# A four-layer graph network: two stages take their blocks from cold to hot, and the next layer's projection gets a queue

## The chip, the cores and the metric

The kernel runs on one core of one Trainium2 chip. The metric is the device time in microseconds of one execution, as the median of several runs. A profile comes from one profiled execution; its span goes from the first to the last instruction of the program.

The engines in the profile: PE (TensorE, matmuls, with PEld for its weight loads), DVE (VectorE), ACT (ScalarE), POOL (GpSimd, which here issues the gathers) and SP (SyncE, which issues the other DMAs).

## What is computed

A graph of 3327 nodes (padded to 3328), 512 features a node, and a sparse 0/1 adjacency matrix. Four layers, each with a residual: layer norm and ReLU, then

- layer 0: graph attention with 8 heads and a batch norm over the nodes,
- layer 1: SAGE, the mean of the neighbours' rows, two projections and a combination,
- layers 2 and 3: graph attention with 8 heads, then ELU.

One attention layer and SAGE, cut from the reference:

```python
h = jnp.maximum(_layernorm(x, axis=-1), 0.0)
# SAGE
agg = mask @ h / jnp.maximum(deg, 1.0)
x = x + relu(concat([h @ W_self + b_self, agg @ W_nb + b_nb]) @ W_comb + b_comb)
# attention
Wh = jnp.einsum('nd,hdo->hno', h, W)
e = leaky_relu(f1[:, :, None] + f2[:, None, :], 0.2)
e = jnp.where(adj[None, :, :] > 0, e, NEG_INF)
x = x + elu(softmax(e, axis=-1) @ Wh)
```

The expected degree of a node falls as one over the square root of its number: the first nodes have many neighbours, the last ones few.

## The kernel before

The nodes are in 26 blocks of 128, each block in two groups of 64 rows. A group has a fixed number of chunks of 128 neighbours, from the table `CAPS`: 22, 15, 13, 12, 11, 10, 9 for the first groups, down to 6 for groups 19 to 29, 5 for 30 to 50 and 4 for group 51. All together 359 chunks. A block with many chunks is called hot here, one with few cold: block 0 has 37 chunks, blocks 15 to 24 have 10 each, block 25 has 9. Block 25 also holds the padded node, whose row stands for a node without neighbours: it is the mean over all nodes (`mean`, L698 to L700), so every other block's row has to be there before it.

The stages follow one another: lists and the first projection, attention 0, batch norm and the first half of SAGE (`own`), SAGE's sums, attention 2, attention 3. Between layers a table in DRAM is written, one row a node, and a small one (`r_dram`) with a factor a node; the next layer's gathers read the table and can only start when all of it is there.

Attention (`attend`): a group's chunks are taken in units of up to three, 135 units a layer. For each unit POOL gathers rows of the table (L1208, one indirect DMA a chunk), DVE makes the weights in two instructions (L1326 and L1333), then `later()` is called, which moves every group's ending on by one step and calls `tick()`, and then PE multiplies the weights with the rows (L1347). At a group's first unit `fetch` loads the factors of the group after next (L1234, on SP) and `spread` broadcasts those of the next one (L1242, on PE). A group's ending takes a copy, a reciprocal and eight multiplications on ACT (L1285); a block's ends with ELU and the residual (`elu_into`, L1378 to L1384), writes x3 and hands the block to the next layer's projection with `begin`.

SAGE's sums: for each block the chunks of its two groups are taken side by side, two a part; POOL gathers `z_rows`, ACT casts the mask, PE adds up (L1612), with one tick per row of chunks. Its ending (`ending(b, acc)`) takes a transpose (L1555), a projection (L1561), and adds `own`'s result in `y` for that block (L1566).

The next layer's projection (`Following`) runs beside both. A block goes through `norm` (three steps, on ACT in attention 2; in SAGE `norm_by_columns`, two steps) in the list `early`, and then through `rest` (six steps: transposes L883 and ReLU L886; sd L891; wh L904; the row and its store L913, L914; a transpose L917; r_row L920 and its store) or, in SAGE, `rest_by_rows` (five steps, L838 to L873) in the list `ready`. In attention 2 all PSUM results of `rest` share one bank (`pb=1`); in SAGE there are two. How many steps a tick takes:

```python
for _ in range(min(2, len(self.ready))):
    while self.ready and next(self.ready[0]) is None:
        self.ready.pop(0)
self.step()
```

so with two blocks ready it takes two steps, and one that finishes a block goes straight on to the next block's first step. After the last unit `hurry` gives the projection spare PSUM banks (those of `mx`), and two blocks move on at a time until all are done.

In both attentions the order on PE, DVE and ACT is that in which the program records its instructions (`manual_schedule`); in SAGE a scheduler orders them. Blocks are taken in the order 0 to 25 everywhere.

Of the kernel before, what the change touches and what calls it, by code (L numbers as in the profile page):

```python
# [23 lines left out]
F32 = mybir.dt.float32  # L24
# [14 lines left out]
P = 128  # L39
H = 8  # L40
F = 64
D = H * F
# [414 lines left out]
class Products:  # L457
# [117 lines left out]
class Projection:  # L575
# [165 lines left out]
class Following:  # L741

    def __init__(self, tc, cs, N, wl, W, WA, table, r_dram, pool, psum, pb=1, ab=None):

        self.__dict__.update(locals())
        nc = tc.nc
        if ab is not None:
            self.ab = pool.tile([P, 2, D], F32, name=f"ab{wl}")  # L750
            for k, a in enumerate(ab):
                nc.sync.dma_start(self.ab[:, k, :], a.partition_broadcast(P))
        self.NB = table.shape[0] // P
        self.Wt = pool.tile([P, KC, D], F32, name=f"fWt{wl}")
        nc.sync.dma_start(self.Wt, W.rearrange("(kc p) o -> p kc o", p=P))
        self.hs = pool.tile([P, self.NB, KC], F32, name=f"hs{wl}")
        self.early, self.ready, self.spare = [], [], None

    def begin(self, c, xt):
        self.early.append((self.norm_by_columns if self.spare is not None or self.ab is not None else self.norm)(c, xt))  # L760

    def busy(self):
        return self.early or self.ready

    def hurry(self, spare):

# [7 lines left out]
    def tick(self):  # L774
        if self.spare is not None:
            for g in self.ready[:2]:
                if next(g) is None:
                    self.ready.remove(g)
            self.step()
            return  # L780
        for _ in range(min(2, len(self.ready))):
            while self.ready and next(self.ready[0]) is None:
                self.ready.pop(0)
        self.step()

    def step(self):
        for g in list(self.early):
            hx = next(g)
            if hx is not None:
                self.early.remove(g)  # L790
                self.ready.append((self.rest if self.ab is None else self.rest_by_rows)(*hx))

    def drain(self):
        while self.early or self.ready:
            self.tick()

    mean = Projection.mean
# [382 lines left out]
def sparse(ctx: ExitStack, tc: tile.TileContext, t: dict, out: bass.AP, WA, ls, cs, idx, rdeg, first):  # L1180
# [17 lines left out]
    x2 = dram.tile([NP, D], F32, name="fx2")  # L1198
    x3 = dram.tile([NP, D], F32, name="fx3")
# [10 lines left out]
        )  # L1210


    def attend(layer, table, r_dram, finish, tick=lambda: None, home=None, beside=None):

# [1 line left out]

        width = table.shape[1]
        units = []  # L1220
        for g in range(ls.G):
            mine = list(ls.batches(g, UNIT))
            units += [(g, k0, n, i == 0, i == len(mine) - 1) for i, (k0, n) in enumerate(mine)]
        hq = H // PG
        sw = hq * (F + 1)
        with tc.tile_pool(name=f"fatt{layer}", bufs=2) as ap, tc.tile_pool(
            name=f"facc_ps{layer}", bufs=2, space=PSUM
# [1 line left out]
            rows, rrs, rbs, accs, ends, over = {}, {}, {}, {}, [], []  # L1229

            def fetch(g):
                if g < ls.G:
                    rr = ap.tile([2, H * GB], F32, name="r_two", tag="r_two", bufs=3)
                    nc.sync.dma_start(rr, r_dram[g, :, :, :].rearrange("t h i -> t (h i)"))  # L1234
                    rrs[g] = rr

            def spread(g):


                if g < ls.G:  # L1240
                    rb = aps.tile([P, H * GB], F32, name="r_bc", tag="r_bc", bufs=2)
                    nc.tensor.matmul(rb, ones[0:2, :].bitcast(F32R), rrs.pop(g).bitcast(F32R), start=True, stop=True)  # L1242
                    rbs[g] = rb.rearrange("p (h i) -> p h i", i=GB)
# [50 lines left out]
                        ends.remove(e)  # L1294
                tick()

            for g in range(2):
                fetch(g)
            spread(0)
            def load(i):  # L1300

                if i >= len(units):
# [18 lines left out]
            for i, (g, k0, n, begins, stops) in enumerate(units):  # L1321
                gt = rows.pop(i)
                mk = mask[:, k0 : k0 + n, :]
                full = [P, n, H, GB]
                mx = aps.tile([P, UNIT, H, GB], F32, name="mx", tag="mx", bufs=1)
                nc.vector.tensor_tensor(  # L1326
                    mx[:, :n],
                    rbs[g].unsqueeze(1).to_broadcast(full),
                    gt[:, :n, H * (F + 1) : ROW].unsqueeze(3).to_broadcast(full),
                    ALU.max,  # L1330
                )
                wt = ap.tile([P, UNIT, H, GB], F32, name="wgt", tag="wgt", bufs=3)
                nc.vector.tensor_tensor(wt[:, :n], mx[:, :n], mk.unsqueeze(2).to_broadcast(full), ALU.mult)  # L1333
                load(i + 1)
                later()
                if begins:
                    fetch(g + 2)
                    acc = aps.tile([P, BANK], F32, name="facc", tag="acc")
                    accs[g] = acc
                    spread(g + 1)  # L1340

                for k in range(n):
                    f, l = begins and k == 0, stops and k == n - 1
                    for q in range(hq):
                        for v in range(PG):
                            h = q * PG + v
                            nc.tensor.matmul(  # L1347
                                accs[g][v * GB : (v + 1) * GB, q * (F + 1) : (q + 1) * (F + 1)],
                                wt[:, k, h, :],
                                gt[:, k, h * (F + 1) : (h + 1) * (F + 1)],  # L1350
                                start=(f and q == 0),
                                stop=(l and q == hq - 1),
                            )
                if stops:
                    ends.append(ending(g))
            over.append(True)
            if beside is not None:
                mx = aps.tile([P, UNIT, H, GB], F32, name="mx", tag="mx", bufs=1)
# [1 line left out]
            while ends or (beside is not None and beside.busy()):  # L1360
                later()

    def following(lx, layer, wl, W, pb=1, ab=None):
# [5 lines left out]
        return Following(tc, cs, N, wl, W, WA, table, r_dram, pp, pps, pb, ab)  # L1369
# [24 lines left out]
    with ExitStack() as mx:  # L1394
# [107 lines left out]
        with tc.tile_pool(name="fln", bufs=1) as bp:  # L1502
# [40 lines left out]
            for i in range(2):  # L1543
                own(NB - 2 + i)

        proj = following(mx, 2, 1, t["L2_gnn_W"], 2, (t["L2_gnn_a1"], t["L2_gnn_a2"]))
        ends = []

        def ending(b, acc):
# [26 lines left out]


        parts = []
        for b in range(NB):
            ps = list(zip_longest(*(list(ls.batches(b * PG + u, SUNIT)) for u in range(PG))))  # L1580
            parts += [(b, p, i == 0, i == len(ps) - 1) for i, p in enumerate(ps)]
        loaded = {}
# [18 lines left out]
        for i, (b, _, begins, stops) in enumerate(parts):  # L1601
# [4 lines left out]
            for r, u, k, m, z in loaded.pop(i):  # L1606
# [3 lines left out]
                g = b * PG + u  # L1610
# [101 lines left out]
```

## Time and profile before

| what | value |
|---|---|
| median of 3 runs | 2906.87 us (2898.61 to 2909.07) |
| span of the profiled execution | 2535.3 us |
| around the span | 371.6 us (difference of the two) |
| PE, DVE, ACT, POOL busy | 73%, 75%, 39%, 56% of the span |
| gathers of SAGE | 919.7 to 1399.0 us |
| units of attention 2 (first L1326 to last L1333) | 1450.4 to 1989.8 us |
| units of attention 3 | 2040.5 to 2513.7 us |

The busy share of an engine over the whole span mixes stages with different limits: each stage has to be read by itself, and the two attentions, which do the same work but for the projection beside the first of them, can be compared unit by unit. In a timeline line the brackets at the end tell how long the engine was idle before it and what ended that.

### The profile page before, as it was taken

How to read it: one execution, taken by the hardware profiler on the slowest of the kernel's cores; microseconds unless marked ns; L12 is line 12 of the kernel's file. 1: busy time of each engine (PE TensorE's matmuls, PEld its weight loads, DVE VectorE, ACT ScalarE, POOL GpSimd, SP SyncE). 2: the span in 40 equal slices, each digit the busy share in tenths (PEclk: the TensorE clock that was granted, in tenths of full speed). 3: DMA queues.
4: the chain of work that ended last, by engine and by line, in shares of the span. 5: the costliest groups of instructions: out<-in, count | busy, mean ns of one | idle time of the engine just before them, and what ended most of it. 6: DMA issues, size and time to landing. Idle time of an engine off the chain costs nothing. (4 is left out here: it accounts for less than half of the span.)

```text
span 2535.3 us, 53563 instructions
## 1 busy us (share of the span) xinstructions
PE 1848.6 (73%) x21112; PEld 1172.1 (46%) x21112; DVE 1901.8 (75%) x2355; ACT 996.7 (39%) x3581; POOL 1427.6 (56%) x1508
## 2 busy tenths in 40 slices
PE   3767756777667698889999667778787746565764
PEld 2444434554444242223333265656555435555654
DVE  7667579999999951233444499999877479999997
ACT  3554212334455431223333114567766501233443
POOL 1000167778776026777776277766555077777663
PEclk9778889988888899999999768898887786778566
DMA  8774188887776566777887478888666178788784
GB/s 327 275 272 132 43 273 281 274 280 217 237 237 196 203 216 203 235 247 256 260 258 243 122 219 239 240 234 238 210 185 198 56 217 234 235 238 244 234 239 129
DMA packets 189056, 562.56 MB, mean 222 GB/s; under 512 B 37764, under 2 KB 42304, under 8 KB 185470
## 3 DMA queue, kind: packets, MB, share of 16 engines
q0 software_dynamic: 115456, 404.86, 53.8%
q1 hardware_dynamic: 73342, 154.20, 17.1%
q8 instruction: 169, 2.77, 0.4%
q14 instruction: 89, 0.73, 0.1%
HBM read 499.26 MB, written 59.68 MB: 220 GB/s over the span
## 5 line engine op out<-in xcount | busy, mean ns | idle before, releaser
L1208 POOL DMA_INDIRECT rows<-table,idx x1077 | 1032.1, 958 | 558.1 <-issue 220.0
L1347 PE MATMUL facc<-rows,wgt 128*64 128x65 f32 x17232 | 744.1, 256 | 346.4 <-DVE wgt L1333 241.2
L1347 PEld LDWEIGHTS facc<-rows,wgt 128*64 128x64 f32 x17232 | 690.0, 168 | 484.5 <-DVE wgt L1333 292.8
L1326 DVE TENSOR_TENSOR mx<-r_bc,rows 128x1536 f32<-128x1536 f32 (+1 forms) x405 | 639.2, 1578 | 40.9 <-DMA rows<-table,idx 23.5
L1333 DVE TENSOR_TENSOR wgt<-mx,mask 128x1536 f32<-128x1536 f32 (+1 forms) x405 | 638.4, 1576 | 41.9 <-ACT bn_y L1285 0.5
L1208 POOL DMA_INDIRECT z_rows<-h_dram,idx x359 | 343.2, 956 | 230.8 <-PE h_ps L1530 94.7
L1285 ACT ACTIVATE fhp<-sums,rd 64x64 f32<-64x64 f32 x816 | 216.0, 336 | 304.1 <-DVE rd L1279 300.8
L1612 PE MATMUL sage_acc<-z_rows,z_mask 128*64 128x512 f32 x718 | 220.2, 620 | 30.8 <-DMA z_rows<-h_dram,idx 30.7
L1318 ACT ACTIVATE mask<-on 128x192 uint8<-128x192 uint16 (+1 forms) x135 | 46.7, 346 | 326.2 <-DVE on L1312 292.7
L849 DVE TENSOR_TENSOR sd_pr<-p_wh,ab 128x1024 f32<-128x1024 f32 x26 | 31.9, 1225 | 187.6 <-PE p_wh L846 187.6
L1129 POOL DMA_DIRECT2D list_b<-shift x12 | 6.0, 506 | 271.7 <-DVE shift L1083 271.5
L1593 ACT CAST z_mask<-mask 128x128 f32<-128x128 uint8 (+1 forms) x196 | 52.8, 287 | 205.3 <-PE sage_acc L1612 204.2
L1612 PEld LDWEIGHTS sage_acc<-z_rows,z_mask 128*64 128x64 f32 x718 | 52.4, 138 | 157.7 <-issue 87.5
L681 PE MATMUL wh_ps<-fWt,hT 128*128 128x512 f32 x208 | 123.5, 749 | 0.0
L1285 ACT ACTIVATE bn_y<-sums,rd 64x64 f32<-64x64 f32 x408 | 107.6, 334 | 1.9
L846 PE MATMUL p_wh<-fWt,hT 128*128 128x512 f32 x208 | 98.6, 618 | 2.1 <-DVE hT L700 1.9
L904 PE MATMUL p_wh<-fWt,hT 128*128 128x512 f32 x184 | 99.9, 691 | 0.0
L1242 PE MATMUL r_bc<-r_two,fones 2*128 2x512 f32 x156 | 94.8, 611 | 7.0 <-DMA r_two<-r_dram 3.4
L1275 ACT COPY sums<-facc 128x260 f32<-128x260 f32 x153 | 55.8, 365 | 105.5 <-PE facc L1347 65.9
L1561 PE MATMUL n_ps<-fWx,aT 128*128 128x512 f32 x208 | 96.8, 605 | 0.2 <-ACT aT L1557 0.2
L1535 PE MATMUL s_ps<-fWx,hT 128*128 128x512 f32 x208 | 93.6, 603 | 3.5 <-ACT hT L1532 3.5
L1044 PE MATMUL words_ps<-wsel,adj_b 128*128 128x8 bf16 x676 | 24.8, 168 | 88.7 <-DVE adj_b L1026 48.4
(232 smaller groups left out, 2146.5 us busy)
## 6 DMA issues: line engine op xcount, KB each, us to landing
adj_i<-in_adj SPq DMA_DIRECT2D x26, 1664.0 KB
table<-v_row SPq DMA_DIRECT2D x78, 264.0 KB
rows<-table,idx POOLq DMA_INDIRECT x1077
fin_x<-fx SPq DMA_DIRECT2D x52, 256.0 KB
ln_x<-in_x SPq DMA_DIRECT2D x26, 256.0 KB
bn_x<-in_x SPq DMA_DIRECT2D x13, 512.0 KB
fx<-bn_x SPq DMA_DIRECT2D x13, 512.0 KB
fsage_x<-fx SPq DMA_DIRECT2D x26, 256.0 KB
```

Source lines behind the costliest of these rows:

```text
L681: nc.tensor.matmul(wh, hT[:, kc, :], self.Wt[:, kc, :], start=(kc == 0), stop=(kc == KC - 1))
L846: nc.tensor.matmul(wh, hT[:, kc, :], self.Wt[:, kc, :], start=(kc == 0), stop=(kc == KC - 1))
L904: nc.tensor.matmul(wh, hT[:, kc, :], self.Wt[:, kc, :], start=(kc == 0), stop=(kc == KC - 1))
L1208: nc.gpsimd.indirect_dma_start(out=dst, out_offset=None, in_=src[:, :], in_offset=bass.IndirectOffsetOnAxis(ap=idx[:, k : k + 1], axis=0))
L1242: nc.tensor.matmul(rb, ones[0:2, :].bitcast(F32R), rrs.pop(g).bitcast(F32R), start=True, stop=True)
L1285: nc.scalar.mul(hp[o0 : o0 + GB, h * F : (h + 1) * F], sm[mine, q, 0:F], rd[mine, q, :])
L1326: nc.vector.tensor_tensor(mx[:, :n], rbs[g].unsqueeze(1).to_broadcast(full), gt[:, :n, H * (F + 1) : ROW].unsqueeze(3).to_broadcast(full), ...
L1333: nc.vector.tensor_tensor(wt[:, :n], mx[:, :n], mk.unsqueeze(2).to_broadcast(full), ALU.mult)
L1347: nc.tensor.matmul(accs[g][v * GB : (v + 1) * GB, q * (F + 1) : (q + 1) * (F + 1)], wt[:, k, h, :], gt[:, k, h * (F + 1) : (h + 1) * (F + 1)],
L1535: nc.tensor.matmul(ps, hT[:, kc, :], Wx[:, 0, kc, :], start=(kc == 0), stop=(kc == KC - 1))
L1561: nc.tensor.matmul(ps, aT[:, kc, :], Wx[:, 1, kc, :], start=(kc == 0), stop=(kc == KC - 1))
L1612: nc.tensor.matmul(acc[u * GB : (u + 1) * GB, :], m, z, start=f, stop=l)
```

## The change

Three things. The blocks of SAGE's sums and of the second attention are taken in the order 24, 23, ..., 0, 25. The projection takes at most two blocks at a time: others wait in a queue and are loaded again from DRAM (`late_x`) when their turn comes. And a tick takes one step of the first ready block only, without going on into the next; attention adds one more step behind the matmuls of every third unit (`beside.onward()`). Attention 0 and attention 3 keep their order.

```diff
+        self.waiting, self.loaded = [], []
 
     def begin(self, c, xt):
+
+        if self.waiting or self.loaded or len(self.early) + len(self.ready) > 1:
+            self.waiting.append(c)
+        else:
+            self.normed(c, xt)
+
+    def normed(self, c, xt):
         self.early.append((self.norm_by_columns if self.spare is not None or self.ab is not None else self.norm)(c, xt))
 
+    def refill(self):
+
+        if self.loaded and len(self.early) + len(self.ready) < 2:
+            self.normed(*self.loaded.pop(0))
+        if self.waiting and not self.loaded:
+            c = self.waiting.pop(0)
+            xt = self.pool.tile([P, D], F32, name="late_x", tag="late_x", bufs=2)
+            self.tc.nc.sync.dma_start(xt, self.xin[c * P : (c + 1) * P, :])
+            self.loaded.append((c, xt))
...
-            self.step()
-            return
-        for _ in range(min(2, len(self.ready))):
-            while self.ready and next(self.ready[0]) is None:
-                self.ready.pop(0)
+        else:
+            self.onward()
         self.step()
+        self.refill()
+
+    def onward(self):
+
+        if self.ready and next(self.ready[0]) is None:
+            self.ready.pop(0)
...
+    late = [*range(NB - 2, -1, -1), NB - 1]
...
-        for g in range(ls.G):
+        order = [b * PG + u for b in blocks for u in range(PG)]
+        after = dict(zip(order, order[1:]))
+        for g in order:
...
-                    fetch(g + 2)
+                    fetch(after.get(after.get(g)))
...
-                    spread(g + 1)
+                    spread(after.get(g))
...
+                if beside is not None and i % 3 == 0:
+                    beside.onward()
...
-        for b in range(NB):
+        for b in late:
...
-        proj = following(l3, 3, 2, t["L3_gnn_W"])
-        attend(2, at2.table, at2.r_dram, elu_into(x2, x3, proj.begin), proj.tick, beside=proj)
+        proj = following(l3, 3, 2, t["L3_gnn_W"], x3)
+        attend(2, at2.table, at2.r_dram, elu_into(x2, x3, proj.begin), proj.tick, beside=proj, blocks=late)
```

More of the change, by code (lines that the diff above doesn't have):

```diff
@@ L741, with __init__ @@
 class Following:
-    def __init__(self, tc, cs, N, wl, W, WA, table, r_dram, pool, psum, pb=1, ab=None):
+    def __init__(self, tc, cs, N, wl, W, WA, table, r_dram, xin, pool, psum, pb=1, ab=None):
         self.__dict__.update(locals())
@@ L757, in __init__ @@
         self.early, self.ready, self.spare = [], [], None
+        self.waiting, self.loaded = [], []
     def begin(self, c, xt):
-        self.early.append((self.norm_by_columns if self.spare is not None or self.ab is not None else self.norm)(c, xt))
+        if self.waiting or self.loaded or len(self.early) + len(self.ready) > 1:
[3 more added lines that the diff above has]
+    def normed(self, c, xt):
+        self.early.append((self.norm_by_columns if self.spare is not None or self.ab is not None else self.norm)(c, xt))
+    def refill(self):
[6 more added lines that the diff above has]
+            self.loaded.append((c, xt))
     def busy(self):
-        return self.early or self.ready
+        return self.early or self.ready or self.waiting or self.loaded
     def hurry(self, spare):
@@ L793, in drain @@
     def drain(self):
-        while self.early or self.ready:
+        while self.busy():
             self.tick()
@@ L1210, in gather, with attend @@
         )
-    def attend(layer, table, r_dram, finish, tick=lambda: None, home=None, beside=None):
+    late = [*range(NB - 2, -1, -1), NB - 1]
+    def attend(layer, table, r_dram, finish, tick=lambda: None, home=None, beside=None, blocks=range(NB)):
         width = table.shape[1]
         units = []
-        for g in range(ls.G):
+        order = [b * PG + u for b in blocks for u in range(PG)]
+        after = dict(zip(order, order[1:]))
+        for g in order:
             mine = list(ls.batches(g, UNIT))
@@ L1231, in fetch @@
             def fetch(g):
-                if g < ls.G:
+                if g is not None:
                     rr = ap.tile([2, H * GB], F32, name="r_two", tag="r_two", bufs=3)
@@ L1237, in spread @@
             def spread(g):
-                if g < ls.G:
+                if g is not None:
                     rb = aps.tile([P, H * GB], F32, name="r_bc", tag="r_bc", bufs=2)
@@ L1295, in later @@
                 tick()
-            for g in range(2):
+            for g in order[:2]:
                 fetch(g)
-            spread(0)
+            spread(order[0])
             def load(i):
@@ L1361, in attend, with following @@
                 later()
-    def following(lx, layer, wl, W, pb=1, ab=None):
+    def following(lx, layer, wl, W, xin, pb=1, ab=None):
         table = dram.tile([NP, ROW], I32, name=f"table{layer}")
@@ L1368, in following @@
         pps = lx.enter_context(tc.tile_pool(name=f"fproj_ps{layer}", bufs=1, space=PSUM))
-        return Following(tc, cs, N, wl, W, WA, table, r_dram, pp, pps, pb, ab)
+        return Following(tc, cs, N, wl, W, WA, table, r_dram, xin, pp, pps, pb, ab)
     def elu_into(xin, dst, then=lambda c, xt: None):
@@ L1544, in sparse @@
                 own(NB - 2 + i)
-        proj = following(mx, 2, 1, t["L2_gnn_W"], 2, (t["L2_gnn_a1"], t["L2_gnn_a2"]))
+        proj = following(mx, 2, 1, t["L2_gnn_W"], x2, 2, (t["L2_gnn_a1"], t["L2_gnn_a2"]))
         ends = []
```

## The prediction

> **What bounds the kernel now.** I read the page, then the busy time by stretch, then the waits of the stretch where the vector engine falls back, and the timeline of one such block. The span is 2535.3 us, the median of the runs 2906.87; the other 371.6 us lie around the span. No part of the change touches them, so I take differences in the span over to the median one to one.
>
> ```profile
> DVE  7667579999999951233444499999877479999997
> ```
>
> Each digit is 63.4 us. The second run of 9s (slices 23 to 27, counted from 0) is attention 2, the third (33 to 38) attention 3; the 8, 7, 7, 4, 7 between them are the hole to look at. By stretch:
>
> ```profile
> core 0: us, PE busy (x) PEld busy (x) DVE busy (x) ACT busy (x) POOL busy (x), PEclk, DMA share, GB/s
> 1740.00:1800.00 60.00, 48.78 (x721) 36.65 (x716) 56.09 (x60) 45.06 (x178) 38.25 (x40) 0.87 0.80 235
> ...
> 1860.00:1920.00 60.00, 48.79 (x632) 35.48 (x629) 44.82 (x55) 42.18 (x167) 30.98 (x32) 0.77 0.62 188
> ...
> 1980.00:2040.00 60.00, 37.81 (x227) 22.35 (x227) 17.67 (x44) 23.50 (x107) 5.80 (x7) 0.73 0.19 69
> 2400.00:2460.00 60.00, 42.84 (x711) 36.74 (x709) 58.36 (x53) 25.52 (x84) 41.98 (x45) 0.64 0.80 235
> ```
>
> The second and the last row are the same work, the coldest blocks, in attention 2 and in attention 3. Attention 3 holds VectorE at 58.4 of 60 us; attention 2 only at 44.8, and no other engine is full. From the starts of L1326 (135 units a layer) each block's period follows: blocks 15 to 24 take 13.7 us in attention 3 and 18.0 to 19.5, mean 18.75, in attention 2; blocks 10 to 14 take 15.8 and 16.8; blocks 0 to 9 together 246.2 and 254.8. So a projection beside costs about 1 us a block where VectorE is the bound (its own small VectorE instructions: 0.15 + 0.27 + 0.16 + 0.17 + 0.16 = 0.91 us), and 5 us in the cold blocks. What is waited for there:
>
> ```profile
> PEld p_ps L883 <- ACT r_row L920: 25.5, 10, 2.7
> ...
> ACT v_row L913 <- PE p_wh L904: 22.3, 10, 2.9
> DVE s_col L901 <- ACT s_col L898: 20.9, 10, 2.5
> ACT v_row L895 <- PE p_sd L891: 18.9, 10, 2.0
> ```
>
> Ten of each, one a block: a ring through PE and ACT, not a full engine. One turn of it:
>
> ```profile
> 1865.95 0.24 ACT L920 COPY r_row<-p_tr 16x128 f32<-16x128 f32 x1
> ...
> 1866.24 1.12 PE L883 MATMUL p_ps<-fident,ln_h 128*128 128x128 f32 x4 [2.51 <-ACT r_row L920]
> ...
> 1868.59 1.89 PE L891 MATMUL p_sd<-WA,hT 128*128 128x16 f32 x8 [1.23 <-ACT hT L886]
> ...
> 1878.87 1.75 ACT L913 ACTIVATE v_row<-p_wh,v_row 128x64 f32<-128x64 f32 x8 [2.86 <-PE p_wh L904]
> ```
>
> r_row, the transposes and sd stand in one tick: with two blocks ready, tick finishes one generator and goes straight on into the next. PE sits in front of attention's matmuls for 2.51 and then 1.23 us, and everything up to the third wgt buffer backs up. The end of attention 2:
>
> ```profile
> 2003.72 6.55 PE L904 MATMUL mx<-fWt,hT 128*128 128x512 f32 x8 [2.45 <-ACT s_col L898]
> ...
> 2014.76 6.16 PE L904 MATMUL mx<-fWt,hT 128*128 128x512 f32 x8 [0.61 <-ACT r_row L920]
> ...
> 2024.90 3.70 PE L904 MATMUL mx<-fWt,hT 128*128 128x512 f32 x8 [0.61 <-ACT r_row L920]
> ```
>
> Three blocks' projections are still to do after the last unit (1989.8), 10.1 to 11.0 us apart; the next layer's first unit starts at 2040.50, 50.7 us later. SAGE:
>
> ```profile
> 1398.08 0.95 POOL L1208 DMA_INDIRECT z_rows<-h_dram,idx  x1 [1.95 <-PE p_tr L869]
> ...
> 1412.26 1.07 PE L1612 MATMUL sage_acc<-z_rows,z_mask 128*64 128x512 f32 x2
> ```
>
> A gather costs GpSimd 0.95 + 0.30 = 1.25 us, and 359 of them make 450 us: this is the pace of SAGE's hot blocks. The cold ones turn PE-bound: the gathers of blocks 20 to 24 are 14.2 us apart instead of 12.5, so PE reaches the last gather's rows 14.2 us after its issue, and the table is complete 28 us after that (write at 1440.46).
>
> **What the Trainium skill says.** "TensorE: Matmul & The Clock Gate", The mechanism: matmuls start and end in strict order. The trace agrees: attention's matmuls stand behind the waiting p_ps. The same page, What's actually happening: the array runs at half clock after about 3.4 us idle and needs as long busy to get back. The trace shows the two speeds (eight matmuls of L904 in 6.55 or 3.70 us, 48 of L1347 in 2.87 or 1.62), so a stall costs more than itself; my forecast uses only these durations. "Trace Analysis", Optimization Strategy: regimes with different contended engines can be interleaved. That is what is tried here, and the window table shows the regimes.
>
> **Part by part, attention 2.** Removed: the double step of tick. In cold blocks before, the steps of four units go 1, 1, 1, 3 (counted from the code: six steps of rest a block, four units). Now it is one a unit plus one behind every third unit's matmuls, 4.5 units a block. A block arrives every 4 units for blocks 24 to 10, every 5 to 13 later, so the queue grows to about four blocks, is at its worst around block 9 and empty by block 4. In the built program's order p_ps always has matmuls of attention between it and p_sd; p_sd and p_wh stand next to each other about once in nine units, where the extra step meets the next tick.
>
> If all 135 units ran at VectorE's pace: attention 3's 473.2 us, 2.5 for the slower first block, and 24 to 25 projections at about 0.95 = 24; sum 500, against 539.4 now. For the remaining stalls: 6 to 7 of 26 sd steps fall on the extra place and make VectorE wait for s_col, nothing to 2.5 us each (the longest such wait shown), so 0 to 16; I take 7, as PE often has the time. 507, a gain of 32. Bounds: 40 (no stall), and 18 if cold blocks only reach 17.0 as the 6-cap blocks do now (10.5 x 1.75).
>
> The projection's PE and ACT work is not less, only moved; in a cold block PE was busy 15.2 us of 18.75 at clock 0.77, ACT 13.2. With 4/4.5 of a projection a block and a warmer clock both fit under 15. That is the cover, and it is thin; without it the 17.0 above holds.
>
> Added: loads of late_x. The order of the built program has 13, all of x3 in attention 2; SAGE gets none, since there five steps meet five ticks a block. 13 x 256 KB is 3.4 MB beside the 200 GB/s moved: hidden. Each waits on SP until the store just issued has landed (a write to a dependent gather took 3.3 us at 1440.46), and behind it stand the r_two fetch, fin_x, the table and r_dram writes. The fetch leads its use by one group, 6.9 us, so I count nothing; with no cover it is 13 x 3 = 39 us. A gain is excluded, nothing is removed there.
>
> **The end of attention 2.** Blocks 0 and 25 are left instead of 23, 24 and 25: the queue is empty through block 0's 13 units. One round of 10 us goes, and PE no longer trails by some 4 us (last facc matmuls ended about 1994.7). Bounds 8 and 14, I take 12. Next in line are block 0's and then block 25's p_wh, unchanged.
>
> **SAGE.** Cold first meets PE while it still has own's matmuls (8.9 us for two blocks, until 961.9). Before, block 0's 37 gathers without any ending let it catch up. Now after 962 some 93 chunks of 5-cap blocks follow, first 13 us light, then at 14.4 a block, and five 6-cap blocks at 15.6: PE at about 1168 there with POOL 13 chunks ahead, and 186 gathers left x 1.254 = 233: last gather about 1401, against 1399. The end gains: a gather's rows can be used about 4 us after its issue (the third gather of attention 2 at 1446.28, its unit at 1450.36), not 14; 10 less 2 is 8. Bounds: 20 gained (the early deficit is absorbed by the buffers), 8 lost (each cold block at 15.5).
>
> Sum: 32 + 12 + 8 = 52 us. 2535.3 becomes 2483, the median 2855.
>
> **Rivals.**
> - Full cover: 40 + 14 + 20 = 74, 2833. For it: six-cap blocks already run within 1 us of VectorE's pace with the 1, 1, 1, 3 pattern. Against: PE and ACT near 13 to 15 us of a 14.7 us block.
> - Half: cold blocks at 17.0, 18 + 10, SAGE 4 lost: 24, 2883. For it: a single PSUM bank (pb=1) keeps the six steps serial.
> - The queue does nothing: the change of order only moves the same stalls to the front, with 10 from the end given back in SAGE: 2900 to 2910. Against it: the program's order shows the p_ps, p_sd pair broken up.
> - Slower: the serial ring through that bank gets longer instead, because each step now waits behind the endings' eight multiplications (2.14 us) on ACT. The queue is then never empty for some 81 units (from the ninth to block 5), each held at ring / 4.5. Blocks 24 to 5 take 369 us now; at a ring of 21.5 us it is 81 x 4.78 + 31 = 418, 49 more, less 20 from the ends: 2936. It decides from 20.7 us on (slower by over 14.5). Now it is 18.75 with a stall of 3.7 in it.
>
> **How the numbers follow.** Forecast 0.52, full cover 0.15, half 0.20, nothing 0.06, slower 0.07. About 0.5% (14.5 us) can be told from no change. Faster 0.87, same 0.06, slower 0.07. The range of 8 in 10 reaches just past full cover and half: 2831 to 2888.
>
> **What would show it.** Right: VectorE above 56 of 60 us in every stretch of attention 2; the 135 units in 500 to 512 us; cold blocks at 14.7 to 15.6; p_ps no longer waiting for r_row by 2.5 us; two L904 groups on mx instead of three, 38 us from last to first unit; SAGE's last gather near 1401 and the last table write near 1432. Wrong: cold blocks at 17 or more, r_bc waiting for r_two behind a late_x load, or SAGE's gathers ending after 1410.

## The result, and the profile after

The changed kernel takes 2909.88 us (median of 20 runs, 2884.17 to 2923.03), the kernel before 2896.53 (20 runs, 2886.26 to 2909.07). The ratio is 1.0035, 95% interval 1.0018 to 1.0053: no gain, and within the 0.5% that the prediction calls no change. 2855 was forecast.

The profile of the changed kernel has a span of 2893.1 us, and the execution it was taken from took 2894.95: next to nothing lies around the span. The profile before had 2535.3 against runs of 2906.87. That is the first thing to explain. The busy digits of VectorE of the changed kernel, each 72.3 us:

```profile
DVE  7758487787787814333321567777776677878886
```

There is no run of 9s any more, not even in attention 0 (slices 5 to 12) and attention 3 (32 to 39), which the change doesn't touch. Attention 3 takes 572.0 us (from its first L1326, here L1351, to the end of its last L1333, here L1358); it was 474.5 in the profile before. By stretch, the changed kernel, two stretches of the coldest blocks in attention 2, one of its hot blocks, one of attention 3's coldest blocks (columns as before: length, busy time and instructions of each engine, PE's clock, share of the DMA engines, GB/s):

```profile
core 0: us, PE busy (x) PEld busy (x) DVE busy (x) ACT busy (x) POOL busy (x), PEclk, DMA share, GB/s
1660.00:1720.00 60.00, 47.99 (x549) 35.28 (x548) 40.71 (x48) 31.68 (x123) 30.56 (x33) 0.69 0.63 179
1720.00:1780.00 60.00, 43.50 (x513) 29.58 (x513) 41.88 (x49) 37.32 (x144) 30.50 (x32) 0.82 0.69 195
...
2200.00:2260.00 60.00, 47.86 (x673) 34.76 (x671) 46.72 (x38) 15.32 (x60) 28.41 (x30) 0.73 0.56 155
2720.00:2780.00 60.00, 43.54 (x602) 34.27 (x602) 49.35 (x45) 22.99 (x74) 36.21 (x38) 0.68 0.71 199
```

VectorE has 41 of 60 us in the cold blocks, and 49 even where no projection runs beside it. What PE waits for tells more. The groups of instructions of PE, attention's matmuls (busy time and mean of one; idle time before them and what ended it), first of the profile before, then of the changed kernel:

```profile
L1347 PE MATMUL facc<-rows,wgt 128*64 128x65 f32 x17232 | 744.1, 256 | 346.4 <-DVE wgt L1333 241.2 <-issue 81.3 <-ACT sums L1275 18.1
```

```profile
L1372 PE MATMUL facc<-rows,wgt 128*64 128x65 f32 x17232 | 970.5, 264 | 443.7 <-issue 407.9 <-DVE wgt L1358 26.3 <-PE r_bc L1267 1.7
```

"Issue" is idle time for which the profile shows no reason. PE waited 241 us for VectorE's weights before and 26 after, and 408 us for nothing visible. Two of the prediction's own signs did come. In attention 2 p_ps no longer waits for r_row: 0.4 us of PE's idle time in all, 31.4 in the profile before. And two rounds of L925 (L904 before) are left at the end. The timeline of the changed kernel:

```profile
2277.92 4.76 PE L925 MATMUL mx<-fWt,hT 128*128 128x512 f32 x8
2284.68 3.70 PE L925 MATMUL mx<-fWt,hT 128*128 128x512 f32 x8 [1.21 <-DVE v_row L929]
```

### The profile page after: what moved, and what is told of

Same layout as the page of the kernel before. It is cut to its first block, busy times and chain, and to the rows that moved or that the text cites. A ratio compares the mean times of both kernels' runs of the same rounds, so it can differ in the third digit from the quotient of the medians.

```text
span 2893.1 us, 53569 instructions
## 1 busy us (share of the span) xinstructions
PE 2096.7 (72%) x21112; PEld 1315.7 (45%) x21112; DVE 1895.4 (66%) x2354; ACT 999.9 (35%) x3589; POOL 1423.8 (49%) x1508
## 5 line engine op out<-in xcount | busy, mean ns | idle before, releaser
L1372 PE MATMUL facc<-rows,wgt 128*64 128x65 f32 x17232 | 970.5, 264 | 443.7 <-issue 407.9
L1372 PEld LDWEIGHTS facc<-rows,wgt 128*64 128x64 f32 x17232 | 820.4, 173 | 666.2 <-issue 593.7
L1358 DVE TENSOR_TENSOR wgt<-mx,mask 128x1536 f32<-128x1536 f32 (+1 forms) x405 | 638.4, 1576 | 154.9 <-PE facc L1372 71.1
L1351 DVE TENSOR_TENSOR mx<-r_bc,rows 128x1536 f32<-128x1536 f32 (+1 forms) x405 | 639.5, 1579 | 132.8 <-PE facc L1372 88.0
L1639 PE MATMUL sage_acc<-z_rows,z_mask 128*64 128x512 f32 x718 | 206.2, 623 | 7.2 <-DMA z_rows<-h_dram,idx 7.2
L925 PE MATMUL p_wh<-fWt,hT 128*128 128x512 f32 x192 | 127.9, 826 | 20.9 <-ACT s_col L919 11.8
L1588 PE MATMUL n_ps<-fWx,aT 128*128 128x512 f32 x208 | 109.7, 658 | 30.8 <-issue 25.4
L867 PE MATMUL p_wh<-fWt,hT 128*128 128x512 f32 x208 | 104.5, 649 | 10.6 <-issue 6.8
L1593 DVE TENSOR_TENSOR s_o<-n_ps,bn_y 128x512 f32<-128x512 f32 x26 | 17.9, 688 | 130.7 <-PE n_ps L1588 62.0
```

What stands on the lines that cost most here:

```text
L867: nc.tensor.matmul(wh, hT[:, kc, :], self.Wt[:, kc, :], start=(kc == 0), stop=(kc == KC - 1))
L925: nc.tensor.matmul(wh, hT[:, kc, :], self.Wt[:, kc, :], start=(kc == 0), stop=(kc == KC - 1))
L1351: nc.vector.tensor_tensor(mx[:, :n], rbs[g].unsqueeze(1).to_broadcast(full), gt[:, :n, H * (F + 1) : ROW].unsqueeze(3).to_broadcast(full), ...
L1372: nc.tensor.matmul(accs[g][v * GB : (v + 1) * GB, q * (F + 1) : (q + 1) * (F + 1)], wt[:, k, h, :], gt[:, k, h * (F + 1) : (h + 1) * (F + 1)],
L1588: nc.tensor.matmul(ps, aT[:, kc, :], Wx[:, 1, kc, :], start=(kc == 0), stop=(kc == KC - 1))
L1639: nc.tensor.matmul(acc[u * GB : (u + 1) * GB, :], m, z, start=f, stop=l)
```

## The experiments

Eighteen runs in five sets; the kernels of one set ran on one chip, beside runs of the kernel before there. Ratios are to those runs.

### First: what the profile before was worth, and the two halves apart

`before_again` is the kernel before; `after_again` the changed one. `steps_only` keeps the queue and the single steps and takes the old order in both stages; `order_only` has the new order and the old projection.

```diff
# steps_only, against the changed kernel
-    late = [*range(NB - 2, -1, -1), NB - 1]
+    late = [*range(NB)]
# order_only, against the changed kernel
     def begin(self, c, xt):
-        if self.waiting or self.loaded or len(self.early) + len(self.ready) > 1:
-            self.waiting.append(c)
-        else:
-            self.normed(c, xt)
+        self.normed(c, xt)
...
-        else:
-            self.onward()
+            self.step()
+            return
+        for _ in range(min(2, len(self.ready))):
+            while self.ready and next(self.ready[0]) is None:
+                self.ready.pop(0)
         self.step()
-        self.refill()
...
-                if beside is not None and i % 3 == 0:
-                    beside.onward()
```

> The kernel before, unchanged, profiled once more. Its first profile has a span of 2535 us beside runs of 2897 us; the changed kernel's has 2893 us beside 2910 us. Theory A (the first profile caught an execution in which PE issued its instructions without pauses, and the timed runs are not like it): span 2870 to 2900 us, PE idle on 'issue' before attention's matmuls some 400 us instead of 81 us, attention 3's units 560 to 580 us instead of 473 us. Theory B (360 us of every run lie around the span): span about 2535 us again, the same 81 us of issue.

> The changed kernel, unchanged, beside the one before on the same chip. Theory A: span 2880 to 2910 us again, or near 2490 us if this execution happens to be one without the pauses; ratio of the runs 1.002 to 1.006. Theory B: span as in its first profile, 2893 us, with almost nothing around it, which B cannot explain for one kernel and not the other.

> The queue and the single steps, with the blocks in the old order 0 to 25 in SAGE and attention 2. If the single steps are what was worth having (the ring through one PSUM bank, as predicted), this is 10 to 30 us below before, less the projections left over at the end (the queue is longest there, one to two blocks more, +10 to +20 us): 2885 to 2905 us. If PE's issue is the bound (theory A), the steps save nothing and the longer end remains: 2905 to 2925 us.

> The new order in SAGE and attention 2, with the old double steps and no queue. By the prediction the end of attention 2 is worth 8 to 14 us and SAGE about 8, the cold blocks nothing: 2875 to 2890 us. If SAGE with the cold blocks first costs more than its end gives back, it is 2900 to 2920 us, and the loss shows between the first gather of z_rows and the last one against before_again.

| run | median us | ratio to before (2867.91), interval |
|---|---|---|
| before_again | 2863.51 | 0.9986 [0.9971, 1.0002] |
| after_again | 2872.88 | 1.0018 [1.0000, 1.0036] |
| steps_only | 2872.23 | 1.0009 [0.9994, 1.0025] |
| order_only | 2849.47 | 0.9919 [0.9883, 0.9955] |

The profile of before_again has a span of 2871.4 us and looks like the changed kernel's: theory A of before_again. The same group of PE there:

```profile
L1347 PE MATMUL facc<-rows,wgt 128*64 128x65 f32 x17232 | 969.9, 264 | 416.2 <-issue 378.8 <-DVE wgt L1333 27.4 <-ACT sums L1275 1.0
```

The timeline of PE in attention 3 of before_again, and below it that of the first profile:

```profile
2716.30 1.91 PE L1347 MATMUL facc<-rows,wgt 128*64 128x65 f32 x26
2718.43 0.50 PE L1347 MATMUL facc<-rows,wgt 128*64 128x65 f32 x4 [0.22 <-issue]
2719.17 0.52 PE L1347 MATMUL facc<-rows,wgt 128*64 128x65 f32 x4 [0.23 <-issue]
```

```profile
2410.46 4.60 PE L1347 MATMUL facc<-rows,wgt 128*64 128x65 f32 x80 [0.98 <-issue]
...
2417.89 1.87 PE L1347 MATMUL facc<-rows,wgt 128*64 128x65 f32 x48 [2.11 <-issue]
```

In the first profile a unit's 48 matmuls go through in one piece. In before_again PE takes four, stands still, and takes four more 0.74 us later; some 26 matmuls on it runs freely again. I call these stops pauses. Between two of attention's matmuls (idle time of 0.15 to 1.3 us) there are 58, 48 us in all, in the first profile, and 741, 353 us in all, in before_again. So the profile that the prediction was worked out from came from an execution unlike the timed ones. On which chip it and the first timed runs were taken is not on record.

The stages (us), from the timelines: SAGE from its first gather to attention 2's first unit, attention 2 from first L1326 to the end of the last L1333, from there to attention 3, attention 3.

| run | SAGE | attention 2 | to attention 3 | attention 3 |
|---|---|---|---|---|
| before_again | 610.1 | 631.7 | 47.0 | 561.2 |
| changed, first profile | 612.0 | 642.8 | 34.8 | 572.0 |
| after_again | 621.3 | 626.2 | 38.2 | 562.0 |
| steps_only | 597.8 | 608.9 | 72.4 | 561.1 |
| order_only | 626.1 | 601.6 | 35.4 | 562.0 |

Either half alone shortens attention 2 by 23 to 30 us; both together by 5.5 in the same set. steps_only gives its 23 us back at the end of attention 2 (72.4 against 47.0). order_only gains what was expected of it, but not where: 30 us in attention 2, where nothing was put down for the cold blocks, and SAGE is 16 longer. These are single executions, and the two of the changed kernel are 17 us apart in attention 2, so only the larger differences count.

### Second: where the changed kernel loses it, and SAGE

`att_order` is order_only with SAGE in the old order. `mix` adds single steps in SAGE alone. `mid_extra` and `clip_moved` are the changed kernel with one edit each: the extra step stands between the first and the second chunk of the unit, not behind its matmuls; VectorE's clip of s_col moves from the step of wh to the start of the step after it.

```diff
# att_order, against order_only
-        for b in late:
+        for b in range(NB):
# mix, against att_order (in tick)
+        if self.ab is not None:
+            self.onward()
+            self.step()
+            return
# mid_extra, against the changed kernel
                 for k in range(n):
+                    if beside is not None and i % 3 == 0 and k == 1:
+                        beside.onward()
...
-                if beside is not None and i % 3 == 0:
-                    beside.onward()
# clip_moved, against the changed kernel
-        nc.vector.tensor_scalar(sf, sf, -SMALL, SMALL, ALU.max, ALU.min)
...
+        nc.vector.tensor_scalar(sf, sf, -SMALL, SMALL, ALU.max, ALU.min)
```

> The kernel before with the new order in attention 2 alone; SAGE keeps 0 to 25, double steps, no queue. Theory A (the gain of the order lies in attention 2 and at its end, SAGE only gives back): against order_only SAGE's 16 us come back. From the stage times of before_again and order_only: attention 2 30 us shorter, its end 12 shorter, SAGE unchanged: 42 us less than before, ratio 0.985, about 2825 where before is 2868. Theory B (SAGE's order moves only what waits, its loss and attention 2's gain are one and the same delay): no better than order_only, ratio 0.992.

> att_order with single steps in SAGE alone (the double steps stay in attention 2, no queue). Theory A (steps_only's 12 us in SAGE come from the single steps there and do not depend on the order): another 10 to 12 us less than att_order, ratio 0.981, about 2813. Theory B (the 12 us were the queue's, which holds blocks back from SAGE's scheduler, or only the spread of single executions): equal to att_order within 0.3%.

> The changed kernel with the extra step of every third unit placed between the unit's first and second chunk instead of behind its matmuls, so that sd and wh do not stand next to each other on PE. Theory A (the neighbourhood of sd and wh, and VectorE's wait for s_col behind it, eat what single steps bring): attention 2 in 600 to 615 us instead of 626 to 643, ratio to before 0.990 to 0.995. Theory B (the queue is the cost: it moves projections from cold blocks to hot ones where each costs more): attention 2 stays at 625 to 640, ratio about 1.002.

> The changed kernel with VectorE's clip of s_col taken one step later, at the start of the step after wh, so that VectorE meets it a unit after sd was issued. Theory A (VectorE's in-order wait for s_col, 82 us idle in after_again against 44 in order_only, is what costs): attention 2 15 to 25 us shorter than in the changed kernel, ratio to before 0.993 to 0.997. Theory B (VectorE only waits there because PE is late anyway; without this wait it waits at the weights' buffers instead): attention 2 within 5 us of the changed kernel's, ratio about 1.002.

The kernel before took 2533.23 us on this chip, and the profiles have no pauses (55 to 65 stops of the kind counted above).

| run | median us | ratio to before, interval |
|---|---|---|
| att_order | 2488.35 | 0.9822 [0.9808, 0.9835] |
| mix | 2488.99 | 0.9822 [0.9808, 0.9837] |
| mid_extra | 2482.45 | 0.9794 [0.9778, 0.9809] |
| clip_moved | 2481.46 | 0.9794 [0.9780, 0.9807] |

All numbers expected were for a chip with pauses, so the first reading is only this: what keeps the changed kernel at 1.00 there may be missing here, or the two edits may have removed it. att_order and mix are equal, in SAGE too (529.2 and 530.6 us): without pauses, single steps bring SAGE nothing. Whether steps_only's 12 us in SAGE were theirs with pauses stays open.

### Third: the changed kernel itself, on a chip without pauses

> The changed kernel unchanged, on whatever chip this call gets. Theory A (there are two kinds of chip: in one PE pauses between instructions all the time and before takes 2860 to 2910 us, in the other it does not and before takes 2533; the sizes of the prediction were those of the second kind): on a chip without the pauses the span is 2480 to 2490, ratio 0.978 to 0.984, attention 2 505 to 512 us, its end 35 us, SAGE 8 to 12 shorter; on a chip with the pauses the ratio is 1.000 to 1.006 again. Theory B (mid_extra and clip_moved were so much faster because of their edits): ratio about 1.00 on either kind.

> att_order again. On a chip with the pauses theory A (the order of attention 2 alone gains, SAGE's order gives back 16 us there): ratio 0.983 to 0.988, about 10 to 16 us ahead of order_only; theory B (SAGE's loss is attention 2's gain in another place): equal to order_only. On a chip without the pauses: 0.982 again.

> mid_extra again, to be set against the changed kernel on the same chip. Theory A (the extra step next to wh makes VectorE wait): on a chip with the pauses 15 to 30 us faster than after_2 (ratio 0.990 to 0.995); on a chip without them the waits are short and it is equal to after_2 within 5 us. Theory B (the queue is the cost): equal to after_2 on either kind.

> The new order in SAGE and attention 2 with the old double steps and no queue. On a chip without the pauses: attention 2 as in att_order, 500 us, its end 36 to 39, SAGE 9 to 12 shorter as in mid_extra: ratio 0.978 to 0.981, so that single steps and queue bring nothing (theory A); theory B (they bring what is missing): behind after_2 by 5 us or more. On a chip with the pauses: 0.992 again, ahead of after_2 by 0.8 to 1.2%.

Another chip, before 2531.00 us, no pauses.

| run | median us | ratio, interval | SAGE | attention 2 | to attention 3 |
|---|---|---|---|---|---|
| before (first profile) | | | 530.7 | 540.8 | 49.4 |
| after_2 | 2483.53 | 0.9812 [0.9799, 0.9826] | 519.2 | 514.7 | 34.5 |
| att_order_2 | 2485.27 | 0.9827 [0.9813, 0.9842] | 529.0 | 506.8 | 35.6 |
| mid_extra_2 | 2474.97 | 0.9784 [0.9769, 0.9800] | 518.7 | 508.7 | 34.7 |
| order_only_2 | 2471.34 | 0.9757 [0.9743, 0.9771] | 518.0 | 506.7 | 35.3 |

This decides it: the change as it stands is 1.9% faster here, 47.5 us, which is theory A of after_2 (its attention 2, 514.7 us, is a little over the 505 to 512 expected), and the edits of mid_extra and clip_moved weren't the reason. The windows of after_2 (columns as above), the coldest blocks of attention 2 and, last, its hot end:

```profile
1460.00:1520.00 60.00, 45.27 (x704) 34.97 (x705) 57.52 (x69) 46.90 (x177) 45.56 (x47) 0.85 0.84 254
...
1820.00:1880.00 60.00, 47.12 (x763) 35.78 (x759) 56.00 (x55) 29.46 (x116) 37.31 (x40) 0.83 0.70 209
```

VectorE is back at 57.5 of 60 us where it had 44.8 before. The order of SAGE gains here: SAGE is 11 us shorter in order_only_2 than in att_order_2.

order_only is 12 us ahead of the changed kernel. The blocks' periods say where (sums in us, from the first instruction of a block to that of the next):

| | blocks 24 to 15 | 14 to 10 | 9 to 5 | 4 to 0 |
|---|---|---|---|---|
| before, no pauses | 184.1 | 84.2 | 100.4 | 154.5 |
| after_2 | 147.3 | 86.2 | 109.2 | 160.6 |
| mid_extra_2 | 147.1 | 85.9 | 109.0 | 155.2 |
| order_only_2 | 149.4 | 85.1 | 105.6 | 155.2 |
| before_again, pauses | 204.6 | 103.6 | 118.1 | 188.3 |
| after_again | 183.9 | 103.3 | 128.5 | 199.1 |
| order_only | 177.8 | 101.8 | 125.2 | 185.4 |

The old double steps break the ring in the cold blocks just as well (149 against 147 us), once the order is turned: counted from the code, the tick's three steps now fall as [tr (the transpose L917), r_row, transposes], and sd comes a unit later, by itself. Before they fell as [r_row, transposes, sd]. The traces agree: on PE the transposes stand right before sd in 14 of 23 blocks of the kernel before, in 1 of 24 of order_only_2. Beside that, the single steps and the queue add only a loss in the hot blocks, which mid_extra takes back in blocks 4 to 0. In attention 2 the single steps and the queue never ran apart from each other, and steps_only was not run without pauses.

### Fourth: mid_extra and att_order again, meant for a chip with pauses

> mid_extra once more, for a chip on which PE pauses between instructions (before takes 2860 to 2910 us). There the changed kernel stands at 1.002 to 1.004 and order_only at 0.992. Theory A (sd and wh next to each other on PE, and VectorE's wait behind them, cost what single steps bring): 0.990 to 0.996, attention 2 in 600 to 618 us. Theory B (the queue moves projections from cold blocks to hot ones, where each costs more): 1.000 to 1.005, attention 2 as in the changed kernel, 626 to 643. On a chip without the pauses: 0.978 to 0.980 for the third time, and the question stays open.

> att_order once more, for a chip with the pauses. Theory A (there SAGE's order gives back the 16 us that the stage times of before_again and order_only show): 0.984 to 0.988. Theory B (SAGE's order costs nothing, the 16 us are spread): 0.991 to 0.994. On a chip without the pauses: 0.982 again.

The chip had no pauses (before 2530.29 us): 2482.31 us, 0.9810 [0.9797, 0.9824], and 2485.37, 0.9809 [0.9792, 0.9826]. mid_extra came out 0.978, 0.979 and 0.981 in three sets, a spread of 6.6 us; its lead over the changed kernel, 9 us in the one set with both, is little more than that. On a chip with pauses neither kernel has run, nor has clip_moved.

### Fifth: a fuller PE in place of pauses

Every matmul of attention's sums is issued twice (numerator and denominator double, the quotient stays).

```diff
-                    for q in range(hq):
-                        for v in range(PG):
+                    for q, again, v in [(q, a, v) for q in range(hq) for a in range(2) for v in range(PG)]:
...
-                                start=(f and q == 0),
-                                stop=(l and q == hq - 1),
+                            start=(f and q == 0 and again == 0),
+                            stop=(l and q == hq - 1 and again == 1),
```

> The kernel before with each matmul of the attentions' sums (facc) issued twice in a row into the same sums; numerators and denominators double, so their quotient is what it was. It adds 17232 matmuls and puts PE where the pauses put it: near or over VectorE's pace. Doubled, a cold unit of 48 matmuls takes 3.2 us (at the 1.62 us that the warm array showed) to 5.7 us (at 2.87), beside VectorE's 3.5. Expected for both theories: attention 3 longer by 20 to 150 us on a chip without the pauses, attention 2 by more, since the projection comes on top. This is the reference for the next three.

> The changed kernel with the same doubling. Theory A (the change loses its gain wherever PE sets the pace of attention, for whatever reason): at most 20 us less than before_twice, attention 2 itself within 10 us of it, where the difference without doubling was 26 to 30. Theory B (it is the pauses as such that take it, each a stall at a bad place; a PE that is merely fuller does not): still 35 us or more below before_twice, attention 2 20 to 30 us shorter.

> mid_extra with the same doubling. Theory A1 (within A: with PE full it is the step that stands next to wh, and VectorE's wait behind it, that costs): 10 to 25 us less than after_twice. Theory A2 (within A: the queue is the cost): equal to after_twice within 5 us.

> order_only, as it was: to be read beside the doubled ones for the difference that single steps and queue make on this chip. Without the pauses 0.976 again (2471 of 2531), with them 0.992.

No pauses again (before 2533.55 us). before_twice 2557.34 us, 1.0100 [1.0082, 1.0119]; after_twice 2517.43, 0.9946 [0.9927, 0.9966]; mid_twice 2513.30, 0.9919 [0.9891, 0.9946]; order_twice (order_only, not doubled) 2475.49, 0.9770 [0.9749, 0.9791]. The group of PE in before_twice:

```profile
L1346 PE MATMUL facc<-rows,wgt 128*64 128x65 f32 x34464 | 1125.8, 227 | 138.4 <-DVE wgt L1333 73.9 <-issue 56.8 <-ACT sums L1275 5.0
```

It was a weak stand-in. PE's clock rose from 0.838 to 0.939, 17232 more matmuls cost 382 us of busy time that mostly took the place of idle time, and attention 3 stayed at 475.3 us, not 20 to 150 longer as expected, where pauses make it 561. 39.9 us of the gain remain (theory B by its number), but in attention 2 only half, 13.6 us (549.9 to 536.3), where theory B has 20 to 30. It shows that a fuller PE alone doesn't take the gain; it doesn't show what PE as the bound would do. mid_twice is 4 us ahead of after_twice in the median, theory A2 by its number and within the spread of the runs; attention 2 is 10 us shorter in the single traces. So the place of the extra step costs little here, if anything.

## Why the prediction was wrong

**The step that failed is the first.** The prediction put it so: "the other 371.6 us lie around the span. No part of the change touches them, so I take differences in the span over to the median one to one." Nothing lies around the span; every profiled execution whose time is on record was within 2 us of its span. The 371.6 us were the difference between an execution without pauses, the one profiled, and the timed ones, which had them, and they lie in the very stages that the change touches. All sizes of the sum belonged to the other kind. On the timed kind, before_again less after_again, attention 2 gains 5.5 us, not 32, its end 8.8, not 12, and SAGE loses 11.2, where 8 were to be gained: 3 us in place of 52.

**Without pauses the sum held, in part by luck.** The span was to become 2483; on a chip without pauses it is 2482.5 us, the median 2483.53. Against runs of the kernel before on the same chip that is 47.5 us, and terms that were too large and too small cancel. Term by term, predicted and measured (the profile before less after_2):
- attention 2: 32 and 26. Cold blocks "at 14.7 to 15.6": 14.7 in the mean, from 18.4 (the prediction read 18.75; block 15 took 16.4). The hot blocks 9 to 0 lost 15 us (254.9 to 269.8). The prediction put down 7 for sd meeting wh, from a count of 6 to 7 in 26. In the trace sd stands right before wh in 12 of 24 blocks; VectorE's wait at the clip, which follows, is 13.4 us in these and 0.2 in the other 12. VectorE was not "above 56 of 60" everywhere: 51.1 to 57.5.
- the end of attention 2: 12 and 15. Two rounds in place of three, 34.5 us.
- SAGE: 8 and 11.5. Last gather at 1396.4, forecast near 1401; last table write at 1428, forecast 1432.
- late_x at no cost: 13 loads, and ACT waited 7.2 us for three of them, with VectorE behind it 0.8 us.

**With pauses the same edits come out otherwise.** The end still gains 9 to 12 us. SAGE gains nothing (2 to 11 us longer). Attention 2's cold blocks gain 21 us instead of 37 (after_again; 16 in the changed kernel's first profile), and its blocks 9 to 0 lose 21 instead of 15 (31 in the first profile). VectorE's idle time in attention 2, by what it went on to do (us, summed from the trace, behind its first instruction of the first unit):

| idle before | no pauses: before | after_2 | order_only_2 | pauses: before_again | after_again | changed, first profile | order_only |
|---|---|---|---|---|---|---|---|
| mx and wgt | 28.4 | 18.8 | 19.2 | 61.9 | 38.9 | 44.4 | 41.4 |
| the clip of s_col | 23.4 | 13.5 | 1.3 | 65.1 | 81.1 | 88.8 | 42.7 |
| the norm's rs_h, rs_g | 11.5 | 5.1 | 12.1 | 25.6 | 26.2 | 30.2 | 37.4 |
| all | 65.0 | 40.8 | 34.4 | 154.3 | 149.7 | 166.2 | 125.3 |

The ring was there with pauses too, but PE stood before sd more than before the transposes (p_ps). PE's idle time before sd that the ReLU of the transposes ended, in attention 2 of before_again and below it of after_again (us, times, longest):

```profile
PE p_sd L891 <- ACT hT L886: 42.7, 18, 4.2
```

```profile
PE p_sd L912 <- ACT hT L907: 8.9, 8, 3.2
```

So the ring went, as foreseen: PE's whole idle time before p_ps and p_sd fell from 66.4 to 21.5 us, and VectorE's waits at the weights by 18 to 23. But the wait for s_col grew by 16 to 24 in its place, and VectorE's idle time as a whole hardly changed. It grew where sd stands right before wh: in after_again VectorE waits 63.4 us in all at those 12 clips and 17.7 at the other 12 (66.6 and 22.2 in the changed kernel's first profile), against 65.1 at 23 clips of before_again, none of which has sd right before wh. One of the 12 in after_again, block 0:

```profile
2218.06 1.76 DVE L1358 TENSOR_TENSOR wgt<-mx,mask 128x1536 f32<-128x1536 f32 x1
...
2218.85 0.35 PE L1372 MATMUL facc<-rows,wgt 128*64 128x65 f32 x4 [0.22 <-issue]
...
2223.13 2.23 PE L1372 MATMUL facc<-rows,wgt 128*64 128x65 f32 x35 [0.45 <-issue]
2225.28 2.00 PE L912 MATMUL p_sd<-WA,hT 128*128 128x16 f32 x8
2228.66 0.17 DVE L922 TENSOR_SCALAR s_col<-s_col 128x8 f32<-128x8 f32 x1 [8.84 <-issue]
2228.68 3.78 PE L925 MATMUL p_wh<-fWt,hT 128*128 128x512 f32 x4 [1.40 <-PE p_sd L912]
2228.84 1.77 DVE L1351 TENSOR_TENSOR mx<-r_bc,rows 128x1536 f32<-128x1536 f32 x1
```

The extra step puts p_sd right before p_wh and its clip. PE comes to p_sd late, behind a unit in which it paused; VectorE, at the clip in its own queue, makes no weights for 8.8 us, and then PE has none either. The prediction had this wait at "nothing to 2.5 us each"; the 12 take 5.3 us each in the mean. Over a whole run, the clip's group in before_again, in after_again and in after_2:

```profile
L901 DVE TENSOR_SCALAR s_col<-s_col 128x8 f32<-128x8 f32 x26 | 4.6, 177 | 68.3 <-ACT s_col L898 51.7 <-ACT v_row L895 9.4 <-issue 7.3
```

```profile
L922 DVE TENSOR_SCALAR s_col<-s_col 128x8 f32<-128x8 f32 x26 | 4.5, 171 | 82.5 <-issue 31.1 <-ACT s_col L919 28.8 <-ACT v_row L916 17.9
```

```profile
L922 DVE TENSOR_SCALAR s_col<-s_col 128x8 f32<-128x8 f32 x26 | 4.9, 190 | 14.9 <-ACT s_col L919 14.9
```

That attention 2's gain is lost at this wait is read from the traces. It wasn't shown by an edit: clip_moved, which takes the wait to 0.0, ran only without pauses, where it left attention 2 at 510.5 us, 4 less than after_2. Why SAGE's gain goes with pauses stays open too.

**The rivals.** "The queue does nothing" came nearest the time, but not by its reason: the pair p_ps, p_sd was broken up, also with pauses. The slower one, a longer ring that makes blocks 24 to 5 take 418 us in place of 369, didn't come: without pauses they take 342.7, and with pauses 415.7 where before_again takes 426.3.

**Better than both:** order_only, the turned order without queue and single steps: 0.9757 and 0.9770 without pauses, 0.9919 with them, ahead of the changed kernel in both sets in which both ran.

## What to carry to other kernels

Set the span of the profiled execution against the timed runs before any size is taken from it: a difference of 372 us between them wasn't time around the program, it was another kind of execution, and a stage that no edit touches (attention 3: 474 against 561 us) tells the two kinds apart. An engine that takes short instructions of another engine's side job in order is only covered as long as that engine comes on time. The waits at the clip speak for putting the producer and the consumer a unit apart; that this pays with pauses was not run here. And before an order, a queue and a step pattern go in together, run each alone: here the order alone came out ahead of all three together, with pauses and without.

## What the hardware showed unexpectedly

The kernel before runs at 2527 to 2539 us (three chips, four sets) or at 2852 to 2909 (one chip of these sets, and wherever the kernels were timed first). Within one set its times lie within 1.1%. On the second kind, in before_again and the changed kernel's first profile, PE pauses in bursts of some 5 us, most of them 5 to 25 us apart, with stops of mostly 0.2 to 0.5 us, most often after four or five matmuls; VectorE's and GpSimd's busy times are the same in both kinds (1895.4 and 1896.1 us of the changed kernel for VectorE).

What makes the pauses is open. The Trainium skill, "Runtime: NRT & Kernel Launch", Instruction fetch mechanics, says that an engine's sequencer fetches its program in blocks of 16 KiB, 256 instructions, and that this is mostly hidden. The profiles agree on the blocks, with the same line for the changed kernel on both kinds:

```profile
q8 instruction: 169, 2.77, 0.4%
```

A packet took 0.97 us (median) in the first profile and 0.98 in before_again. In attention 3 of before_again a pause begins between 0.3 us before and 1 us after 28 of 45 packets (62%), and in the same way around 60% of instants taken at even distances (44% and 56% in after_again). So the traces show no tie between fetch and pauses. Nor do they for the clock: "TensorE: Matmul & The Clock Gate", What's actually happening, has the clock follow PE's activity, and it did so when the matmuls were doubled (0.838 to 0.939), but between the two kinds it differs little (0.838 in the first profile, 0.802 in before_again, with 256 and 264 ns a matmul in the mean), while the stops between matmuls go from 48 to 353 us.
